# Unread products of the identity on TensorE between the steps of a rotation

## The chip, the cores and the metric

The kernel runs on one core of a Trainium2 chip. The metric is the device time of one execution in microseconds; the median of three runs of the kernel before is 2110.49 us. One execution was also recorded by the profiler.

## The reference

The input x has the shape 4 x 512 x 288, the condition 4 x 288, all in float32. Four blocks are computed in turn:

- a rotation: U is the Q of a QR decomposition of P (288 x 64); per batch a skew matrix is made from silu(cond) @ W.T + b, and its matrix exponential R (64 x 64) rotates the part of x that lies in the span of U: x + ((x U) R - x U) U^T;
- two transformer blocks with modulation by the condition (layer norm, attention with 16 heads of 18, a feed-forward of 1152), the second with a layer norm of each head's queries and keys;
- a third one whose feed-forward is a mixture of four experts, of which each token uses two.

The change lies in the first block and in the start of the first attention.

## The kernel before

**The QR decomposition** is an elimination of 64 steps on the Gram matrix, written out as a Python loop over columns (lines 560 to 576). Two chains run in it. `gram_step(i)` copies row i of X to all 64 partitions by a product with one column of the identity (`to_all`, g_bc), and VectorE makes from it the reciprocal rn, the multipliers Fm and the update of X; ScalarE takes a root (Nm) and GpSimd a product (Rh). `sign_step(i)` does the same with row i of Wt (w_bc) and fixes the signs: six small operations of VectorE, of which the last writes Wt. The loop calls gram_step(i + 1) ahead of to_all and sign_step(i), so that g_bc runs one column ahead. Both rows are put into tiles of PSUM with the tag "big": two banks wide, two buffers in all, used in turn. Of each tile only the first bank is used here.

**Beside it** the loop advances three generators. `main` (`skew_and_exp`) transposes W (p_WT), multiplies (p_v), builds the skew matrices, and from column 33 on runs nine steps of a series (p_ser) and sixteen squarings (p_sq), one per column, each a group of 64 x 64 products and one operation of VectorE. `side` transposes x (p_t), projects it (p_zP), and later does the first modulations (p_mod, p_modT). `fills` clears buffers. In the whole loop the instructions keep the order of the program on each engine. TensorE takes its products in that order.

**Behind the loop** p_E and p_Q finish Q; `rotate(0)` applies the rotation to batches 0 and 1 in six parts (p_RU, p_EU, and four times p_xr with VectorE's sums into x). `head_biases(0)` makes bias columns (p_qkb). `normalize` computes the layer norm of batch 0 on VectorE and ScalarE, `project(0)` transposes and makes queries, keys and values (p_t, p_qk, p_v), with parts of `rotate(1)` between, and sends queries and keys through memory into the layout of heads. Then ten steps of `maxima` (LOOK = 10) run ahead of the attention's loop: each makes two products p_s of 32 rows by 512 columns in one "big" tile, and VectorE takes their maximum. The last parts of `rotate(1)` lie between these steps. The attention's loop, the feed-forwards and the experts follow.

A dependence between engines is a wait on a semaphore that counts the finished instructions of an engine. An instruction of TensorE that waits holds all that stand behind it.

Of the kernel before, what the change touches and what calls it, by code (L numbers as in the profile page):

```python
# [33 lines left out]
D = 64  # L34
# [13 lines left out]
def cond_seq_kernel(ctx: ExitStack, tc: tile.TileContext, a: dict, out: bass.AP):  # L48
# [16 lines left out]
    matmul, transpose = InOrder(nc.tensor).matmul, InOrder(nc.tensor).transpose  # L65
# [10 lines left out]
    blocks = ctx.enter_context(ExitStack())  # L76
    fixed = blocks.enter_context(tc.tile_pool(name="fixed", bufs=1))

    def pmm(name):
        return ps.tile([128, 512], F32, tag="mm", name=name, bufs=3)  # L80

    def pbig(name):
        return ps.tile([128, 2, 512], F32, tag="big", name=name)

    def pacc(name):
        return ps.tile([128, 512], F32, tag="acc", name=name, bufs=1)
# [17 lines left out]

    ident = const.tile([128, 128], F32, name="ident")
    make_identity(nc, ident)
    ones = const.tile([1, 128], F32, name="ones")
    nc.gpsimd.memset(ones, 1.0)
    eps6 = const.tile([128, 1], F32, name="eps6")
# [60 lines left out]
    def to_columns(name, r):  # L170

        p = pmm(f"p_{name}")
        for m in range(NQ):
            w = min(QP, QK - m * QP)
            matmul(p[0:w, m:m + 1], r[:, m * QP:m * QP + w], ones[:, 0:1], start=True, stop=True)
        t = const.tile([QP, NQ], F32, name=name)
        nc.gpsimd.memset(t, 0.0)
        scalar.copy(t[:, 0:NQ - 1], p[0:QP, 0:NQ - 1])
        scalar.copy(t[0:w, NQ - 1:NQ], p[0:w, NQ - 1:NQ])
        return t  # L180
# [21 lines left out]
    def head_biases(l):  # L202
        QB[l] = to_columns(f"qkb{l}", WA[l][3])
        if l != 1:
            vector.tensor_mul(QB[l], QB[l], scol)
# [155 lines left out]
    with tc.tile_pool(name="l0", bufs=1) as l0, tc.tile_pool(name="l0w", bufs=2) as l0w, \  # L361
# [24 lines left out]
        Hs = l0.tile([D, D], F32, name="Hs")  # L386

        def to_all(name, i, src):
            p = pbig(name)[:D, 0, :src.shape[-1]]
            matmul(p, ident[:D, i:i + 1].to_broadcast([D, D]), src, start=True, stop=True)  # L390
            return p

        def gram_step(i):
            bc = to_all(f"g_bc{i}", i, X[:, i:i + D + 1])
            rn = l0w.tile([D, 1], F32, tag="rn", name=f"rn{i}")
            vector.reciprocal(rn, bc[:, 0:1])
            vector.scalar_tensor_tensor(Fm[:, i:i + 1], X[:, i:i + 1], rn, minus[:, i:i + 1], ALU.mult, ALU.mult)
            vector.scalar_tensor_tensor(X[:, i + 1:i + D + 1], bc[:, 1:], Fm[:, i:i + 1],
                                        X[:, i + 1:i + D + 1], ALU.mult, ALU.add)
            scalar.activation(Nm[:, i:i + 1], bc[:, 0:1], AF.Sqrt, scale=0.25)  # L400
            nc.gpsimd.tensor_mul(Rh[:, i:i + 1], Fm[:, i:i + 1], Nm[:, i:i + 1])

        def sign_step(i, bc):

            h = Hs[:, i:i + 1]
            vector.tensor_scalar(h, bc[:, 0:1], 0.0, 0.5, ALU.is_lt, ALU.subtract)
            if i == D - 1:
                return
            st = l0w.tile([D, 4], F32, tag="st", name=f"st{i}")
            den, rec, num, c = (st[:, n:n + 1] for n in range(4))  # L410
            vector.tensor_scalar(den, bc[:, 0:1], h, Nm[:, i:i + 1], ALU.mult, ALU.subtract)
            vector.scalar_tensor_tensor(num, Wt[:, i:i + 1], h, Rh[:, i:i + 1], ALU.mult, ALU.add)
            vector.reciprocal(rec, den)
            vector.scalar_tensor_tensor(c, num, rec, minus[:, i:i + 1], ALU.mult, ALU.mult)
            vector.scalar_tensor_tensor(Wt[:, i + 1:], bc[:, 1:], c, Wt[:, i + 1:], ALU.mult, ALU.add)
# [145 lines left out]
        for i in range(D):  # L561
            column[0] = i
            if i + 1 < D:
                gram_step(i + 1)
            bc = to_all(f"w_bc{i}", i, Wt[:, i:])
            beside = i >= 6 and (i < 15 or i >= 18)
            next(main, None)
            if beside:
                next(side, None)
            sign_step(i, bc)  # L570
            next(main, None)
            if beside:
                next(side, None)
            next(fills, None)
            if i == 27:

                WA.append(load_attn(0, "L1_cond_W_qkv", "L1_cond_b_qkv", "L1_cond_W_proj", "L1_cond_b_proj"))
# [17 lines left out]
                                    Hs.rearrange("p (o d) -> p o d", o=1).to_broadcast([D, B, D]), ALU.mult, ALU.mult)  # L595
        pt = pmm("p_Q")
        matmul(pt[:D, :C], Em, At, start=True, stop=True)
        vector.tensor_scalar_mul(QT, pt[:D, :C], rnorm)
        scalar.copy(XD, X[:, D:])


    def rotate(n):

        ts = []
        for h in range(2):
            p = pmm(f"p_RU{2 * n + h}")
            matmul(p[:D, :C], Es[:, 2 * n + h, :], QT, start=True, stop=True)
            t = work.tile([128, C], F32, tag="gated", name=f"RU{2 * n + h}", bufs=3)
            scalar.mul(t[:D], p[:D, :C], rnorm)
            ts.append(t)  # L610
        yield 0.6
        e = work.tile([128, C], F32, tag="gate", name=f"EU{n}")
        p = pmm(f"p_EU{n}")
        for h in range(2):
            matmul(p[h * D:(h + 1) * D, :C], XD, ts[h][:D], start=True, stop=True)
        scalar.copy(e, p[:, :C])
        yield 0.6
        for j in range(NT):
            ps = pmm(f"p_xr{2 * n}_{j}"), pacc(f"p_xr{2 * n + 1}_{j}")
            for h in range(2):  # L620
                r = slice(h * D, (h + 1) * D)
                matmul(ps[h][:, :C], zP[r, n, j * 128:(j + 1) * 128], e[r], start=True, stop=True)
            for h in range(2):
                xb = x[2 * n + h][:, j, :]
                vector.tensor_add(xb, ps[h][:, :C], xb)
            yield 0.6
# [6 lines left out]
    def normalize(l, part, b, after=None):  # L633


        xn = []
        mv = work.tile([128, NT, 2], F32, tag="mv", name=f"mv{l}_{part}_{b}")
        for j in range(NT):
            while after is not None and (after, j) not in done:
                yield False  # L640
            s6 = work.tile([128, 6], F32, tag="s6", name=f"s6_{l}_{part}_{b}_{j}", bufs=4)
            vector.bn_stats(s6, x[b][:, j, :])
            vector.bn_aggr(mv[:, j, :], s6)
            yield True

        r = work.tile([128, 2, NT], F32, tag="rstd", name=f"rstd{l}_{part}_{b}")
        y, t, var = r[:, 0, :], r[:, 1, :], mv[:, :, 1]
        scalar.activation(y, var, AF.Ln, bias=eps6)
        scalar.activation(y, y, AF.Exp, scale=-0.5)
        yield True  # L650
        vector.scalar_tensor_tensor(t, var, 1e-6, y, ALU.add, ALU.mult)
        vector.tensor_mul(t, t, y)
        vector.tensor_scalar(t, t, -0.5, 1.5, ALU.mult, ALU.add)
        vector.tensor_mul(y, y, t)
        yield True
        for j in range(NT):
            t = work.tile([128, C], F32, tag="xn", name=f"xn{l}_{part}_{b}_{j}", bufs=8)
            vector.tensor_scalar(t, x[b][:, j, :], mv[:, j, 0:1], y[:, j:j + 1], ALU.subtract, ALU.mult)
            xn.append(t)
            yield True  # L660
        XN[l, part, b] = xn
# [345 lines left out]
    with tc.tile_pool(name="attn", bufs=2) as at:  # L1007
# [90 lines left out]
        def maxima(G, step):  # L1098

            n, g = divmod(G, NG)  # L1100
            j, hp = divmod(step, 2)
            p = pbig(f"p_s{G}_{step}")
            for i in range(2):
                r = slice((2 * hp + i) * HS, (2 * hp + i + 1) * HS)
                matmul(p[:, i, :], Q[n % 2][r, g, j * 128:(j + 1) * 128], K[n % 2][r, g, :], start=True, stop=True)
            vector.tensor_reduce(M[G % 2][:, j, 2 * hp:2 * hp + 2, HD:HD + 1], p, AX.X, ALU.max)
# [155 lines left out]
            yield from route(b)  # L1262

        E, ready, PO, S, there, norms = [], [], [None], {}, set(), {}
        for _ in rotate(0):
            pass
        head_biases(0)
        norm = normalize(0, 0, 0)
        for _ in norm:
            pass  # L1270
# [3 lines left out]
        for cost in project(0, norm):  # L1274
            next(norm1, None)
            sent = sent or cost is None
            if sent and cost == 0.95:
                next(rest, None)
        norm = norm1
        for t in range(LOOK):  # L1280
            maxima(*divmod(t, 8))
            if t == 8:
                take_maxima(0)
            next(norm, None)
            next(rest, None)
# [212 lines left out]
```

## Time and profile before

| | |
|---|---|
| median of 3 runs | 2110.49 us (2103.7 to 2111.6) |
| the profiled execution | 2122.64 us, span 2120.9 us |
| TensorE busy | 1933.4 us, 91% of the span |
| VectorE busy | 933.8 us |
| ScalarE busy | 777.1 us |
| mean granted clock of TensorE | 0.933 |
| columns of the rotation | 7.6 us (first reciprocal) to 148.6 us (last w_bc) |
| first product of maxima | 194.8 us |

A row of the timeline has the start and the length in us, the engine, the line, the operation, what it writes and reads, rows and columns of the array, the shape, and the number of instructions merged; in brackets the idle time of the engine just before it and what ended that. Nearly all instructions are recorded at line 60, that of a helper, so groups are read by the names of tiles. A product in float32 is recorded as two MATMULs, one per pass; a transpose as one. The granted clock is 1.00 at full and 0.50 at half speed.

### The profile page before, as it was taken

Reading aid. Unit: us, or ns where it says so; the run is one execution under the profiler, and the core shown is the slowest. Engines: PE = TensorE matmul, PEld = TensorE weight load, DVE = VectorE, ACT = ScalarE, POOL = GpSimd, SP = SyncE. Lnnn points to the kernel's source line nnn. Section 1 sums busy time; section 2 is a strip of 40 time slices with the busy share of each in tenths; the row PEclk is TensorE's granted clock in tenths of the full one; section 3 lists DMA queues with packets and bytes.
Section 4 is the critical chain, followed back from the end, with each engine's and each line's share of the span. In section 5 each row is a group of like instructions: output and inputs, shape, how many; then the busy total and the mean of one; then the engine's idle time right before and its main releaser. Section 6 shows DMA issues by size and latency. Waiting matters only on the chain. (4 is left out here: it accounts for less than half of the span.)

```text
span 2120.9 us, 26102 instructions
## 1 busy us (share of the span) xinstructions
PE 1933.4 (91%) x10200; PEld 936.0 (44%) x10200; DVE 933.8 (44%) x1974; ACT 777.1 (37%) x1159; POOL 251.3 (12%) x361
## 2 busy tenths in 40 slices
PE   7778989999999999899999999998987899999997
PEld 4553322343433434334234343333322367777775
DVE  6774535526256263552643626355577134111111
ACT  5111444434345354443543434434444222112111
POOL 1000001000001020110100000000010122332322
PEclk9556899999999999989999999999999689999999
DMA  3211125122031121511213112161221355666563
GB/s 95 70 39 45 34 65 160 26 56 76 16 75 41 52 79 45 127 46 25 88 27 77 48 51 81 21 135 31 81 51 58 111 196 178 203 207 223 182 216 94
DMA packets 89418, 187.21 MB, mean 88 GB/s; under 512 B 25453, under 2 KB 50456, under 8 KB 86802
## 3 DMA queue, kind: packets, MB, share of 16 engines
q1 hardware_dynamic: 77462, 103.39, 18.8%
q0 software_dynamic: 11248, 79.79, 11.6%
q10 hardware_dynamic: 584, 2.36, 0.4%
q8 instruction: 80, 1.31, 0.3%
q14 instruction: 44, 0.36, 0.1%
HBM read 152.49 MB, written 55.45 MB: 98 GB/s over the span
## 5 line engine op out<-in xcount | busy, mean ns | idle before, releaser
L60 ACT ACTIVATE e<-p_st 128x1024 f32<-128x1024 f32 x384 | 392.7, 1023 | 692.1 <-PE p_st L60 687.8
L60 DVE TENSOR_REDUCE store<-p_s 128x2 f32<-128x1024 f32 x384 | 470.2, 1225 | 385.1 <-PE p_st L60 334.0
L60 PE MATMUL p_s<-store 32*128 32x512 f32 x1536 | 452.6, 664 | 79.7 <-DVE store L60 76.9
L60 PE MATMUL p_st<-store 32*128 32x512 f32 x1536 | 449.8, 664 | 0.9 <-DVE store L60 0.9
L60 PEld LDWEIGHTS p_s<-store 32*128 32x128 f32 x1536 | 122.7, 190 | 312.5 <-DVE store L60 221.4
L60 PE MATMUL p_av<-e,store 128*32 128x512 f32 x1536 | 213.5, 629 | 2.2 <-ACT e L60 2.2
L60 PE MATMUL p_he<-hTe,store 128*128 128x256 f32 (+1 forms) x1026 | 200.1, 404 | 4.2 <-DVE hTe L60 4.2
L60 PE MATMUL p_ye<-store,hide 128*128 128x288 f32 x684 | 175.0, 415 | 7.1 <-ACT hide L60 7.1
L60 ACT ACTIVATE hide<-p_he,store 128x256 f32<-128x256 f32 x171 | 68.5, 471 | 281.8 <-PE p_he L60 281.8
L60 PEld LDWEIGHTS p_he<-hTe,store 128*128 128x128 f32 (+1 forms) x1026 | 147.6, 191 | 53.1 <-issue 30.5
L691 POOL TENSOR_TENSOR x<-x,gated 128x288 f32<-128x288 f32 x80 | 63.4, 793 | 848.0 <-DVE gated L60 848.0
L60 PE MATMUL p_qk<-hT,wqk 128*126 128x512 f32 (+1 forms) x360 | 163.9, 626 | 0.0
L60 PE MATMUL p_h<-hT,w 128*128 128x512 f32 (+1 forms) x432 | 156.7, 618 | 5.2 <-DVE store L60 5.2
L60 PEld LDWEIGHTS p_ye<-store,hide 128*128 128x128 f32 x684 | 130.3, 193 | 46.9 <-ACT hide L60 10.9
L60 PE MATMUL p_y<-w,hid 128*128 128x288 f32 x576 | 141.8, 407 | 0.0
L60 DVE TENSOR_TENSOR gated<-p_y,gate 128x288 f32<-128x288 f32 x32 | 14.6, 457 | 285.8 <-PE p_y L60 285.8
L60 PEld LDWEIGHTS p_st<-store 32*128 32x128 f32 x1536 | 119.5, 189 | 12.4 <-issue 9.3
L60 PEld LDWEIGHTS p_y<-w,hid 128*128 128x128 f32 x576 | 108.8, 190 | 35.5 <-issue 6.1
L60 PEld LDWEIGHTS p_h<-hT,w 128*128 128x128 f32 (+1 forms) x432 | 60.7, 189 | 99.7 <-issue 83.6
L60 PE MATMUL p_o<-wp,oc 126*128 126x288 f32 (+1 forms) x288 | 101.2, 475 | 1.3 <-DVE oc L60 1.3
L60 PEld LDWEIGHTS p_qk<-hT,wqk 128*126 128x126 f32 (+1 forms) x360 | 47.8, 179 | 98.7 <-issue 98.5
L60 DVE COPY hTe<-p_te 128x512 f32<-128x512 f32 x19 | 13.1, 690 | 172.9 <-PE p_tf L60 127.8
(248 smaller groups left out, 1736.6 us busy)
## 6 DMA issues: line engine op xcount, KB each, us to landing
store<-qd SPq DMA_DIRECT2D x96, 144.0 KB
qd<-stage SPq DMA_DIRECT2D x48, 252.0 KB
od<-o SPq DMA_DIRECT2D x192, 36.0 KB
rd<-rd SPq DMA_DIRECT2D x12, 576.0 KB
oc<-od SPq DMA_DIRECT2D x24, 252.0 KB
rb<-rd SPq DMA_DIRECT2D x24, 252.0 KB
etab<-in_L_cond_w_dram SPq DMA_DIRECT2D x4, 1296.0 KB
etab<-in_L_cond_w_dram SPq DMA_DIRECT2D x8, 576.0 KB
```

Of the source, the lines that this page charges most:

```text
L60: ins = f(*args, **kw)
L691: nc.gpsimd.tensor_add(x[b][:, j, :], x[b][:, j, :], t)
```

## The change

A function `keep_warm(bank, n)` multiplies the identity by the identity, taken up to four times side by side, and writes n columns (in pieces of at most 512) to a bank of PSUM that nothing reads. It is called

- in each column of the loop, behind sign_step and the generators, with 384 or 256 columns, into the second bank of the tile that holds w_bc;
- behind p_Q (256), behind each part of rotate(0) (256), behind head_biases(0) (five of 512);
- in project(0) behind two pieces of the values (512), and once behind it (512);
- behind each of the ten steps of maxima (128, from the sixth on 256), into a tile of the tag "mm".

```diff
+    def keep_warm(bank, n):
+
+        while n > 0:
+            w = min(n, 512)
+            matmul(bank[:, :w].rearrange("p (o m) -> p o m", m=128), ident, ident_wide[:, :w // 128, :], start=True, stop=True)
+            n -= w
...
+    ident_wide = ident.rearrange("p (o m) -> p o m", o=1).to_broadcast([128, 4, 128])
...
         def to_all(name, i, src):
-            p = pbig(name)[:D, 0, :src.shape[-1]]
+            t = pbig(name)
+            p = t[:D, 0, :src.shape[-1]]
             matmul(p, ident[:D, i:i + 1].to_broadcast([D, D]), src, start=True, stop=True)
+            free[0] = t[:, 1]
             return p
+
+        free = [None]
...
             bc = to_all(f"w_bc{i}", i, Wt[:, i:])
             beside = i >= 6 and (i < 15 or i >= 18)
+            warm = free[0]
             next(main, None)
             if beside:
                 next(side, None)
...
+            keep_warm(warm, 384 if i < 3 or i >= 52 or 29 <= i < 33 else 256)
             next(fills, None)
...
         matmul(pt[:D, :C], Em, At, start=True, stop=True)
+        keep_warm(pbig("warm0")[:, 0], 256)
         vector.tensor_scalar_mul(QT, pt[:D, :C], rnorm)
...
+        warm = pbig("warm1")
         for _ in rotate(0):
-            pass
+            keep_warm(warm[:, 0], 256)
         head_biases(0)
+        keep_warm(warm[:, 0], 5 * 512)
...
             if sent and cost == 0.95:
                 next(rest, None)
+                keep_warm(warm[:, 1], 512)
+        keep_warm(warm[:, 1], 512)
         norm = norm1
         for t in range(LOOK):
             maxima(*divmod(t, 8))
+            keep_warm(pmm(f"warm2_{t}"), 256 if t > 4 else 128)
```

## The prediction

> **What bounds the kernel now.** I read the page's rows of forty slices first, then the busy time by stretches of the opening, then the timeline of single columns. Each slice is 53 us.
>
> ```profile
> PE   7778989999999999899999999998987899999997
> PEclk9556899999999999989999999999999689999999
> ```
>
> TensorE is busy nearly everywhere, and the granted clock is low in the second to fourth slice, that is in the rotation and just behind it. Nothing before or behind the opening is touched by the change, so the opening is read by stretches. The columns are the length, then PE, PEld, DVE, ACT and POOL busy, then the clock.
>
> ```profile
> 29.00:46.20 17.20, 14.84 (x107) 7.89 (x109) 13.90 (x78) 7.57 (x21) 1.66 (x12) 1.00 0.13 38
> 46.20:80.00 33.80, 25.21 (x108) 13.50 (x100) 25.84 (x145) 9.02 (x28) 2.93 (x16) 0.50 0.45 110
> 80.00:148.00 68.00, 51.18 (x563) 39.65 (x563) 55.36 (x293) 9.03 (x45) 7.10 (x34) 0.50 0.13 31
> 149.00:176.00 27.00, 19.87 (x53) 10.04 (x54) 12.13 (x46) 6.15 (x15) 0.00 (x0) 0.50 0.00 0
> 196.40:227.00 30.60, 28.94 (x78) 9.16 (x76) 17.69 (x22) 1.23 (x2) 0.26 (x1) 0.50 0.00 1
> ```
>
> The reader is to see that the clock is at half for 130 us (46.2 to 175.9) and again for 31 us, though TensorE is shown busy for 75% and 95% of those stretches. Which of this costs time is a second question. In the rotation (64 columns, 7.6 to 148.6) VectorE does nine small operations per column, and the timeline of one column shows who waits:
>
> ```profile
> 142.93 0.21 DVE L60 SCALAR_TENSOR_TENSOR Wt<-w_bc,st,Wt 64x4 f32<-64x4 f32 x1
> 143.06 0.15 DVE L60 RECIPROCAL rn<-g_bc 64x1 f32<-64x1 f32 x1
> 143.29 0.34 PE L60 MATMUL w_bc<-Wt,ident 64*64 64x4 f32 x2 [0.49 <-DVE rn L60]
> ...
> 144.08 0.48 PE L60 MATMUL g_bc<-X,ident 64*64 64x65 f32 x2 [0.45 <-ACT Nm L60]
> ...
> 144.69 0.21 DVE L60 SCALAR_TENSOR_TENSOR Wt<-w_bc,st,Wt 64x3 f32<-64x3 f32 x1
> 144.83 0.15 DVE L60 RECIPROCAL rn<-g_bc 64x1 f32<-64x1 f32 x1
> ```
>
> The broadcast row g_bc for the next column is computed at 144.08, while VectorE is still in the sign step; so when Wt ends at 144.90 the reciprocal rn has its input and follows at once (1.77 us from rn to rn). Even at half clock TensorE's round trip is under VectorE's work. In columns that also add a series or squaring result the step is 2.1 us, again all VectorE. Over the 62 steps from the second to the last rn (8.99 to 146.64) 137.7 us pass; the waits of rn on g_bc sum to 12.3 us in the whole rotation. So a faster TensorE has at most about 12 us to win there. What happens if g_bc is late is seen where long products stand ahead of it:
>
> ```profile
> 63.17 1.97 PE L60 MATMUL p_zP<-xT,hT 96*64 96x512 f32 x4
> ...
> 65.08 0.47 PE L60 MATMUL g_bc<-X,ident 64*64 64x65 f32 x2
> 65.59 0.16 DVE L60 RECIPROCAL rn<-g_bc 64x1 f32<-64x1 f32 x1 [0.59 <-PE g_bc L60]
> ```
>
> g_bc starts as p_zP is through, and VectorE idles for it: rn follows 0.51 us behind g_bc's start.
>
> **The change part by part.**
>
> **The 64 products in the rotation.** Each writes the second bank of the tile whose first bank holds w_bc(i), and is emitted behind sign_step(i). In the instruction list of the changed program each such product waits for a VectorE count, and the count is that of Wt(i), the last reader of w_bc(i): the wait is kept per tile, not per bank. Behind it in TensorE's queue stands g_bc(i+2), whose own wait (on ScalarE's Nm) is met long before. So g_bc(i+2), which before ran during sign_step(i), now runs behind the end of sign_step(i) and behind the product. rn, X, w_bc(i+1) and all the rest of the column wait for that.
>
> The price of a product comes from the weight loads of p_qk, one per pass of 512 columns, two passes per product, on either side of the clock's change at 175.9:
>
> ```profile
> 174.51 0.34 PEld L60 LDWEIGHTS p_qk<-hT,wqk 128*126 128x126 f32 x1 [0.52 <-issue]
> 175.36 0.34 PEld L60 LDWEIGHTS p_qk<-hT,wqk 128*126 128x126 f32 x1 [0.52 <-issue]
> ...
> 176.51 0.19 PEld L60 LDWEIGHTS p_qk<-hT,wqk 128*126 128x126 f32 x1 [0.24 <-issue]
> 176.94 0.19 PEld L60 LDWEIGHTS p_qk<-hT,wqk 128*126 128x126 f32 x1 [0.24 <-issue]
> ```
>
> A pass takes 0.85 us at half clock and 0.43 at full. A product of 256 columns is then 0.85 or 0.43 us, of 384 1.28 or 0.64, of 512 1.71 or 0.86. The new round trip from the end of Wt to rn: 0.15 until TensorE starts (Wt ends 142.93+0.21, w_bc at 143.29), the product, g_bc 0.47 (0.33 at full clock, at 30.79), 0.04 to rn. That is 1.51 us at half clock, 0.95 at full. From rn to the end of Wt VectorE needs 1.84 (143.06 to 144.90). A column becomes 3.35 us at half clock, 2.79 at full; with 384 columns 3.78 and 3.00. The series and squaring results (0.40), the products for them and the other work on TensorE now lie beside this round trip and cost nothing more; if it were gone they would cost what they cost before.
>
> **Does the clock rise?** The nearest rows are TensorE's own. From 196.4 to 227 it is busy 95% of the time with products on 64 of 128 rows and stays at half. From 60.7 to 67.6 p_zP (96 rows) runs about 80% of the time and the clock does not rise. It rose at 29 (four p_WT took 1.07 us before, 0.64 behind; no clock is on record before that) behind six us of 126- and 128-row transposes that filled about 85% of each column, and at 175.9 behind dense p_t and p_qk; it was lost at 46.2 in columns whose p_v uses 4 array columns. At half clock a column with a 256 product has 0.85 of 3.35 us of whole array and the series' products on a quarter of it, worth about 0.45 us more: 1.3 of 3.35, near 0.4 of the array, less than the stretches that stayed low. The Trainium skill's page "TensorE: Matmul & The Clock Gate" (Part 1) counts otherwise: a busy window of about 3.4 us gives full clock, and only an idle one of that length takes it away. By that rule TensorE, with no idle gap above 1.5 us between 46 and 149, should have been at full clock already; the trace has 0.50 there. I take the trace: full clock in some five columns after 29 us as before, half in the rest. By the rule it would be full clock from the tenth column on.
>
> By the trace: 45 columns of 256 at 3.35 = 151, 17 of 384 at 3.78 = 64, five columns at full clock -3, the column with the modT transposes +2: 214 against 137.7, +76 us. By the rule: 45 x 2.79 + 17 x 3.00 = 177, the first nine at half clock +6, +1: 184, +46 us.
>
> **Behind the rotation.** The last two products of 384 stand ahead of w_bc(63) and of p_E: +3 us at half clock. warm0 and the six products between rotate(0)'s parts fill gaps of 0.5 us (waits on QT, RU, EU and the sums) and stick out by about 0.35 each, the last by its whole 0.85: +3 (at full clock all of this is -2 with the chain's own products halved). The five of 512 stand where TensorE waits from 165.1 to 169.8 for the normalization: 4.3 us at full clock fit; at half clock 8.5 would stick out by 4, but p_xr just ahead (two side by side fill the array, with the new ones between near 0.8 of the time) and these five themselves raise the clock. Then p_t and p_qk up to 175.9 start at full clock: -2. The three of 512 beside the second rotation: +1.7, less 0.8 idle: +1. Maxima:
>
> ```profile
> 200.66 1.33 PE L60 MATMUL p_xr<-EU,hT 64*128 64x288 f32 x4
> 200.81 1.23 DVE L60 TENSOR_REDUCE store<-p_s 128x2 f32<-128x1024 f32 x1 [1.23 <-PE p_s L60]
> 201.93 2.08 PE L60 MATMUL p_s<-store 32*128 32x512 f32 x4
> ```
>
> Four steps of 3.27 us (p_xr and p_s at half clock) fall to VectorE's 2.1 (the maximum 1.23 and two sums 0.82) at full clock with 128 columns added; the six behind win 2, p_bv and the first p_st 3: -9. If the clock is not held here it is +4 instead.
>
> Sum: 76 + 3 + 3 - 2 + 1 - 9 = +72 on the profiled execution's 2122.6 us (2120.9 of span): 2195. That execution was 12.1 us above the median of the runs, 2110.5: **2183** there.
>
> **The rivals.**
>
> **Full clock through the rotation.** For it: the widths are larger exactly where TensorE has least to do, and it was held from 29 to 46 with about 0.35 of the array. Against it: 0.23 to 0.3 of the array at full clock in the later columns, less than where it was lost. It gives 46 + 1 - 2 - 2 + 1 - 9 = +35: 2145.
>
> **Hidden products, and the clock held: faster.** If the products ran in the gap between g_bc and w_bc (0.5 to 0.66 us in the timeline, against 0.43 for 256 columns) the column would stay as it is, rn's 12.3 us of waits would shrink by perhaps 8, and with -6 on the chain from p_Q to the sums and -10 behind it this would be -24: 2087. It needs a product that is free to start before Wt(i) has ended, or an exposed round trip of under 0.39 us a column (24 over 62). Against it: the wait on Wt(i) in the instruction list, and the order of the queue, in which nothing behind a blocked product can start.
>
> **The change does nothing.** The added waits and the clock's gains cancel, or the round trip lies beside other VectorE work: only in the 26 series columns is there any, 0.40 us. Little speaks for it.
>
> **How the numbers follow.** Half clock in the rotation 0.65 (2168 to 2203), full clock through most of it 0.23 (2130 to 2165), faster 0.08, no change 0.04. The range 2134 to 2203 leaves out about the last two and a corner of the second. About 0.5% (11 us) is what a measurement of this kernel can tell from no change. Slower 0.88, same 0.04, faster 0.08.
>
> **What would show it.** rn should wait on g_bc in all columns, 0.9 to 1.6 us each, 50 to 90 us in total instead of 12.3; w_bc's product should wait on Wt; the last rn should stand at 200 to 230 us (half) or near 190 (full) instead of 146.6; the clock at half in most of it and at full from the normalization to past the maxima; maxima every 2.1 us in the first four steps. A last rn near 140 would make the prediction wrong, and so would a clock of 0.5 over the maxima, in size.

## The result, and the profile after

The changed kernel takes 2190.43 us (median of 4 runs, 2185.02 to 2198.64), against 2109.15 us before (4 runs): ratio 1.0386, 95% interval 1.0344 to 1.0427. The forecast was 2183, with a range of 2134 to 2203. In the rows below PE is TensorE and PEld its weight loads, DVE is VectorE, ACT ScalarE and POOL GpSimd.

The rows of the forty slices (55 us each now) show the low clock in the second to fifth slice, one more than before:

```profile
PE   6778899899999999989999999999997889999998
PEclk9655699899999999999999999999999989999999
```

The stretches of the opening, cut where the clock changes (columns as in the prediction; the first entry is the stretch, the last two are the DMA engines' share and GB/s):

```profile
43.70:74.40 30.70, 22.74 (x144) 11.60 (x142) 17.39 (x95) 9.60 (x27) 1.84 (x11) 1.00 0.05 17
74.40:160.00 85.60, 63.33 (x330) 35.32 (x330) 42.00 (x224) 7.07 (x29) 4.79 (x25) 0.50 0.17 43
160.00:240.00 80.00, 61.11 (x408) 34.98 (x405) 38.39 (x198) 8.48 (x36) 4.86 (x23) 0.50 0.11 26
240.00:255.30 15.30, 14.76 (x34) 5.74 (x33) 3.18 (x12) 1.84 (x5) 0.00 (x0) 0.50 0.00 0
255.30:289.00 33.70, 33.45 (x113) 14.91 (x112) 11.21 (x40) 9.93 (x20) 0.00 (x0) 1.00 0.25 69
289.00:311.00 22.00, 22.00 (x96) 8.76 (x96) 16.23 (x21) 0.00 (x0) 0.26 (x1) 1.00 0.01 2
```

The rotation now runs to 240, not 148.6, and from 74.4 on at half clock. VectorE's share is what to look at: 38.4 of 80 us, where it had 55.4 of 68. It waits. Two rows of the waits between 9 and 237 us say for whom:

```profile
DVE rn L60 <- PE g_bc L60: 100.3, 63, 2.9
PEld w_bc L60 <- DVE Wt L60: 79.8, 61, 2.2
```

The numbers are the total in us, the number of waits and the longest. The kernel before had, between 9 and 148 us:

```profile
DVE rn L60 <- PE g_bc L60: 12.1, 21, 2.0
```

So rn waited in 21 columns, and now it does in every one. (The second row above is the weight load of the product, which writes a tile named w_bc.) The timeline of one column in the series, at half clock; "..." stands for rows left out:

```profile
152.68 0.23 DVE L60 SCALAR_TENSOR_TENSOR Wt<-w_bc,st,Wt 64x23 f32<-64x23 f32 x1
152.84 0.41 DVE L60 SCALAR_TENSOR_TENSOR ser<-p_ser,S 128x256 f32<-128x256 f32 x1
152.97 0.50 PEld L60 LDWEIGHTS w_bc<-ident 128*128 128x128 f32 x2 [1.09 <-DVE Wt L60]
152.97 1.22 PE L60 MATMUL w_bc<-ident 128*128 128x256 f32 x2 [0.90 <-DVE Wt L60]
...
154.12 0.47 PE L60 MATMUL g_bc<-X,ident 64*64 64x65 f32 x2
...
154.63 0.16 DVE L60 RECIPROCAL rn<-g_bc 64x1 f32<-64x1 f32 x1 [1.39 <-PE g_bc L60]
```

Wt ends at 152.91, the product starts 0.06 us later, g_bc starts 1.15 us later, rn 0.51 us behind that. TensorE had been idle for 0.90 us ahead of the product: the gap is there, but the product can't use it.

From 289 on, the maxima, at full clock:

```profile
294.57 1.23 DVE L60 TENSOR_REDUCE store<-p_s 128x2 f32<-128x1024 f32 x1 [0.18 <-PE p_s L60]
...
295.56 1.13 PE L60 MATMUL p_s<-store 32*128 32x512 f32 x4
...
296.73 1.23 DVE L60 TENSOR_REDUCE store<-p_s 128x2 f32<-128x1024 f32 x1 [0.21 <-PE p_s L60]
```

One step is 2.16 us, where it was 3.27. From the first p_s to the first exponential the changed kernel takes 22.0 us, the one before 31.0.

By landmarks, after against before, in us: last rn +89.9, p_E +93.3, the first statistics of the normalization +94.5, first p_v +92.3, first p_s +94.3, first exponential +85.3. The two profiled spans differ by 62.4 only; the other 23 were won back behind the first exponential, where the change adds nothing. There the clock's record has 126 us at half clock in the profiled execution of before and 80 in that of the changed kernel; half of these 46 us is 23 (an estimate that takes all of that work to wait for TensorE). Executions of one kernel differ by such amounts: four of the changed one span 2183.3 to 2196.9, and the profiled one is the shortest, while that of before was 12 us above its median. The medians differ by 81.3.

### The profile page after: what moved, and what is told of

Read it like the earlier page. It is cut to its first block, busy times and chain, and to the rows that moved or that the text cites. A ratio compares the mean times of both kernels' runs of the same rounds, so it can differ in the third digit from the quotient of the medians.

```text
span 2183.3 us, 26392 instructions
## 1 busy us (share of the span) xinstructions
PE 1981.5 (91%) x10378; PEld 958.6 (44%) x10378; DVE 935.9 (43%) x1974; ACT 776.6 (36%) x1159; POOL 251.0 (11%) x361
## 5 line engine op out<-in xcount | busy, mean ns | idle before, releaser
L60 PE MATMUL p_s<-store 32*128 32x512 f32 x1536 | 440.9, 646 | 79.5 <-DVE store L60 77.3
L60 PE MATMUL p_st<-store 32*128 32x512 f32 x1536 | 439.7, 649 | 0.9 <-DVE store L60 0.9
L60 PE MATMUL p_he<-hTe,store 128*128 128x256 f32 (+1 forms) x1026 | 200.2, 405 | 4.2 <-DVE hTe L60 4.2
L60 PEld LDWEIGHTS p_he<-hTe,store 128*128 128x128 f32 (+1 forms) x1026 | 147.8, 191 | 53.1 <-issue 30.6
L60 PE MATMUL w_bc<-ident 128*128 128x256 f32 (+1 forms) x128 | 80.9, 732 | 55.3 <-DVE Wt L60 55.1
L60 PE MATMUL p_o<-wp,oc 126*128 126x288 f32 (+1 forms) x288 | 91.5, 438 | 1.3 <-DVE oc L60 1.3
```

The source lines that it names most:

```text
L60: ins = f(*args, **kw)
```

## The experiments

All times are medians; the ratios are to runs of the kernel before on the same chip.

**behind: the loop's products left out.**

```diff
-            keep_warm(warm, 384 if i < 3 or i >= 52 or 29 <= i < 33 else 256)
```

> The changed kernel without the 64 products inside the columns of the rotation; all products behind it stay. Queue theory (a product waits for Wt, and g_bc of the next column stands behind it): the last rn is back at 146.6 us, the products from p_Q to the bias columns cost 1 us, the maxima win 9 us by the full clock, so about 2101 us, 0.4% under the 2109 of before. Rival (the products behind the rotation share the loss): over 2115 us.

Measured: 2103.49 us (12 runs), ratio 0.9981 (0.995 to 1.0011); the last rn at 145.5, the first exponential 9.7 us earlier than before. So the whole loss lies in the loop; the products behind it shorten their stage, but by less than the totals resolve, as the interval takes in 1. The stretch from the first p_s to the first exponential, before and here:

```profile
194.80:225.80 31.00, 29.60 (x75) 9.22 (x76) 16.49 (x21) 0.03 (x1) 0.26 (x1) 0.53 0.03 7
```

```profile
194.10:216.00 21.90, 21.90 (x96) 8.73 (x96) 16.21 (x20) 0.00 (x0) 0.26 (x1) 1.00 0.00 1
```

**loop_only: only the loop's products.**

```diff
-        keep_warm(pbig("warm0")[:, 0], 256)
...
-            keep_warm(warm[:, 0], 256)
+            pass
...
-        keep_warm(warm[:, 0], 5 * 512)
...
-                keep_warm(warm[:, 1], 512)
-        keep_warm(warm[:, 1], 512)
...
-            keep_warm(pmm(f"warm2_{t}"), 256 if t > 4 else 128)
```

> Only the 64 products inside the columns; none behind the rotation. Queue theory: the last rn stays at 236.6 us, the first p_s finds half clock again, the ten maxima take 31 us as before, so about 2109 + 90 = 2199 us. Rival (what lies behind costs too): under 2180 us.

Measured: 2202.18 us (4 runs), ratio 1.0441 (1.0389 to 1.0493); last rn at 234.6; from the first p_s to the first exponential 29.8 us at a mean clock of 0.59. With behind it splits the change: about +94 from the loop, -5 to -12 from the rest.

**narrow: the same wait and place, two columns.**

```diff
-            keep_warm(warm, 384 if i < 3 or i >= 52 or 29 <= i < 33 else 256)
+            matmul(warm[:, :2], ident, ident[:, :2], start=True, stop=True)
```

> The products inside the columns write 2 columns instead of 256 or 384; place and wait stay, and all behind the rotation stays. Queue theory: g_bc still starts only behind the end of Wt, so a column is 1.84 (VectorE) + 0.15 + 0.35 (two short passes with their weight loads) + 0.51 (g_bc to rn) = 2.85 us; last rn near 186 us, in all about 2109 + 39 - 8 = 2140 us. Rival (the loss is TensorE's time for the products, not the wait): last rn near 147 us, in all about 2101 us.

Measured: 2154.21 us (4 runs), ratio 1.0236 (1.0179 to 1.0292); last rn at 200.2, +54. With next to no columns streamed through the array, more than half of the loss is there. This execution ran its whole rotation at half clock (its p_v take 1.02 us, against 0.59 at full), where the kernel before had 17 us at full, so a small part of the 54 may be the clock's: the three columns with p_v take 4.03 us, the others near 3.0. A column of it:

```profile
143.50 0.23 DVE L60 SCALAR_TENSOR_TENSOR Wt<-w_bc,st,Wt 64x20 f32<-64x20 f32 x1
...
143.87 0.50 PEld L60 LDWEIGHTS w_bc<-ident 128*128 128x128 f32 x2 [0.96 <-DVE Wt L60]
143.88 0.59 PE L60 MATMUL w_bc<-ident 128*128 128x2 f32 x2
...
144.39 0.47 PE L60 MATMUL g_bc<-X,ident 64*64 64x65 f32 x2
...
144.91 0.16 DVE L60 RECIPROCAL rn<-g_bc 64x1 f32<-64x1 f32 x1 [0.85 <-PE g_bc L60]
```

g_bc starts 0.51 us behind the start of a product of two columns. That is two weight loads of the identity (0.50 in the timeline), and the expectation had 0.35 for the whole of it. This column takes 3.06 us, most take 2.94 to 3.00, and the mean of 62 is 3.08; expected were 2.85, hence 2154 instead of 2140.

**free: the same products, waiting for nothing.**

```diff
+                keep_warm(p[:, 4 * D:], 256)
                 return p[:, :4 * D]
...
-            keep_warm(warm, 384 if i < 3 or i >= 52 or 29 <= i < 33 else 256)
+            if i < 34 or i >= 59:
+                keep_warm(pacc(f"free{i}"), 384 if i < 3 or i >= 52 or 29 <= i < 33 else 256)
```

Up to column 33 only the tile differs from the changed kernel: width and place in the order are the same. From column 34 on the product stands behind the series' or squaring products, in their bank.

> The products inside the columns keep their widths (256 in place of 384 in columns 52 to 58) but write the accumulator's bank, alone up to column 33, then beside the series' products, so that none waits for VectorE. Queue theory: the columns without much other work go back to near 2 us, those with transposes or projections stay near 3.6 as TensorE at half clock is full there; last rn 165 to 185 us, in all 2120 to 2140 us. Rival (TensorE's time for the products is the loss, the wait adds nothing): last rn 215 to 237 us, over 2170 us.

Measured: 2124.95 us (9 runs), ratio 1.0086 (1.0054 to 1.0119); last rn at 164.8, +18. The wait of rn on g_bc is 16.9 us in all, and g_bc no longer follows Wt through a product:

```profile
142.71 1.22 PE L60 MATMUL p_sq<-ident 128*128 128x256 f32 x2
...
143.34 0.22 DVE L60 SCALAR_TENSOR_TENSOR Wt<-w_bc,st,Wt 64x10 f32<-64x10 f32 x1
...
143.86 0.29 PEld L60 LDWEIGHTS g_bc<-X,ident 64*64 64x64 f32 x2 [0.65 <-issue]
143.97 0.42 DVE L60 SCALAR_TENSOR_TENSOR sq<-sq,p_sq 128x256 f32<-128x256 f32 x1 [0.41 <-PE p_sq L60]
...
144.37 0.16 DVE L60 RECIPROCAL rn<-g_bc 64x1 f32<-64x1 f32 x1
```

The product starts ahead of Wt's end, so a column is 2.78 us instead of 3.59. The first 33 columns are the cleanest comparison: rn of column 33 starts at 77.2 before, at 78.2 here and at 121.8 in the changed kernel. So the same products cost 1 us without the wait and 45 with it; full clock, which stands here from 21.2 to 72.4, helps by a part of that. What is left of the loss comes later, where TensorE at half clock has no idle time left, and the squaring result, which shares the product's tile, waits for it:

```profile
126.70:165.00 38.30, 38.04 (x267) 25.10 (x266) 27.59 (x138) 3.82 (x22) 3.77 (x17) 0.50 0.12 28
```

Between 120.2 and 127.0 the clock was at full once more; the two columns that start there, at 121.8 and 124.0, took 2.13 and 3.90 us, no longer than before (2.54 and 4.21).

**swap: g_bc ahead of the product** (`width` gives 384 or 256 as the removed line does).

```diff
-        def gram_step(i):
+        def gram_step(i, behind=None):
             bc = to_all(f"g_bc{i}", i, X[:, i:i + D + 1])
+            if behind is not None:
+                keep_warm(behind, width(i - 2))
...
-                gram_step(i + 1)
+                gram_step(i + 1, warm)
+            else:
+                keep_warm(warm, width(i - 1))
...
-            keep_warm(warm, 384 if i < 3 or i >= 52 or 29 <= i < 33 else 256)
...
+        keep_warm(warm, 384)
         for _ in main:
```

> The changed kernel with each product of the rotation one place later in TensorE's order: behind g_bc of the next column but one, ahead of the next w_bc. Width and the wait for Wt stay. Queue theory: g_bc runs early again and rn follows Wt; now w_bc stands behind the product, 0.15 + 1.15 + 0.35 us after Wt, where VectorE needs it 0.65 to 0.9 us after Wt, so a column at half clock is 1.65 + 1.20 = 2.9 us (3.4 with 384), about 3.9 with transposes; last rn near 205 us, in all about 2160. Rival (the place in the queue is of no weight, the product's own time is): last rn at 230 us or more, 2185 or more.

Measured: 2166.7 us (5 runs), ratio 1.0296 (1.0242 to 1.035); last rn at 210.6. One place in the order is worth 26 us of the rotation, with the same products, the same wait and as long a full clock (31 us of the rotation in both). The size of the gain was overrated by a few us: in the columns with modulations rn waits after all.

```profile
152.20 1.22 PE L60 MATMUL w_bc<-ident 128*128 128x256 f32 x2
...
153.48 0.29 PE L60 MATMUL w_bc<-Wt,ident 64*64 64x19 f32 x1
...
153.92 0.15 DVE L60 TENSOR_SCALAR Hs<-w_bc 64x1 f32<-64x1 f32 x1 [0.89 <-PE w_bc L60]
...
155.80 0.48 PE L60 MATMUL g_bc<-X,ident 64*64 64x65 f32 x2
...
156.31 0.16 DVE L60 RECIPROCAL rn<-g_bc 64x1 f32<-64x1 f32 x1 [0.83 <-PE g_bc L60]
```

Hs waits for the w_bc that stands behind the product, as expected. But p_sq and p_mod stand behind that w_bc, and the next g_bc behind them: rn waits 0.83 us more, and the column is 4.0 us.

**lift: 2560 columns in four columns of the rotation.**

```diff
-            keep_warm(warm, 384 if i < 3 or i >= 52 or 29 <= i < 33 else 256)
+            keep_warm(warm, 5 * 512 if 34 <= i < 38 else 384 if i < 3 or i >= 52 or 29 <= i < 33 else 256)
```

> The changed kernel with 2560 columns instead of 256 in columns 34 to 37 of the rotation, to raise the clock there; all else as in the changed kernel. Theory that the clock follows how much of the array is used: it rises in the first or second of these columns, and is lost within 7 us after column 38, as columns of 256 use about a quarter of the array at full clock; columns from 40 on take 3.6 us again, last rn near 250 us. Rival (a busy window raises the clock and only an idle one takes it away): full clock to the end of the rotation, columns of 2.95 us, last rn near 233 us.

Measured: 2223.84 us (one run); last rn at 261.2, where 250 was expected. Ten of these 11 us lie ahead of the first wide column: column 34 starts at 135.8, and at 125.8 in the changed kernel, though up to there the two are the same program; here the first 34 columns all ran at half clock (more on this below). The clock's record begins with the rise at 147.4, inside the first wide column, and has the loss at 174.7. The wide columns at full clock, what follows until the loss, and the half clock behind:

```profile
147.40:169.50 22.10, 17.97 (x101) 8.51 (x101) 5.87 (x30) 0.49 (x3) 0.55 (x3) 1.00 0.00 1
169.50:174.70 5.20, 2.45 (x41) 1.83 (x39) 3.92 (x20) 0.33 (x2) 0.37 (x2) 1.00 0.00 0
174.70:205.00 30.30, 28.01 (x215) 15.47 (x214) 15.59 (x80) 3.88 (x16) 1.47 (x8) 0.50 0.15 35
```

A wide column takes 6.78 us, of which ten passes of 0.43 fill the whole array, 0.63 of the time. The columns of 256 behind them (the first takes 2.93 us) lose the clock 5.2 us later, with TensorE shown busy for 47% and no idle gap above 1.4 us. So in this one execution the products of the change were too few to hold the clock in these columns, even once it was there.

**maxima_only: only the products beside the values and the maxima.**

```diff
-            keep_warm(warm, 384 if i < 3 or i >= 52 or 29 <= i < 33 else 256)
...
-        keep_warm(pbig("warm0")[:, 0], 256)
...
-            keep_warm(warm[:, 0], 256)
+            pass
...
-        keep_warm(warm[:, 0], 5 * 512)
```

> Only the products beside the values, behind the projection and in the ten steps of maxima; none in or ahead of rotate(0) and none at the bias columns. Queue theory: the rotation and the chain behind it take the time of before; the clock, at full by the projection's own products, is held over the maxima, which take 9 us less; about 2099 us against 2108, and 1 us better than with the products from p_Q on. Rival (the products at the bias columns are what brings the clock to the maxima): half clock there and no gain.

Measured: 2104.75 us (12 runs), ratio 0.9972 (0.9937 to 1.0006). The clock was held:

```profile
196.90:218.80 21.90, 21.90 (x96) 8.73 (x96) 16.22 (x21) 0.00 (x0) 0.26 (x1) 1.00 0.00 1
```

The first exponential comes 6.9 us earlier than before; of the 9 us of the maxima, the three products of 512 ahead of them cost 1.9 (the first p_s is 2.1 late). The products from p_Q to the bias columns win about 1.5 us more: in behind the first exponential is 9.7 us earlier than before, but 1.1 of that is there at the last rn already, where the two kernels are the same. The rival expectation, that the clock needs the products at the bias columns, is out. The expectation that those products cost 1 us was wrong in sign, though by less than the totals of behind and this run (2103.49 and 2104.75) can tell. Neither version is told from the kernel before by its total; both beat the changed one.

## Why the prediction was right

**The wait and the order** (right). The prediction's step was that the product waits for Wt and g_bc stands behind it, so that the round trip comes onto the path. The product writes the second bank of its tile and Wt reads the first, and yet 61 weight loads of the product waited for Wt (79.8 us). narrow (the wait with almost no streaming, +54 us at the last rn), free (the streaming without the wait, +18, and only 1 of the 45 us up to column 33) and swap (-26 by one place in the order) show it, each with its own edit. rn waits in every column: 1.05 us in those at full clock, 1.39 to 1.82 in most at half, 2.15 in most of those with 384, and 100 us in all. Forecast were 0.9 to 1.6 each and 50 to 90 in all.

**The column's size** (0.25 us too small at half clock, 0.16 at full). 3.60 and 2.95 us were measured, 3.35 and 2.79 forecast. The term that was mis-sized is the product: 0.85 us was taken from the spacing of p_qk's passes, where the weight loads lie beside the stream before them. Here nothing streams before them, and 1.15 us pass from the start of the product to that of g_bc, 0.30 more; at full clock it is 0.63 instead of 0.43. The start of the product was misread the other way: the 0.15 us from Wt to w_bc in the prediction's timeline lie ahead of a product that waited for rn, as its bracket says, and the start behind Wt took 0.06. Over 52 steps at half clock and ten at full this makes about 15 us too little; longer columns (the first of 4.97, those with p_mod of 3.69) add about 2, and five more columns at full clock than forecast take 3 off. Together they are the 14 us by which the rotation's forecast of +76 fell short of +90.

**The clock** (right in its choice, half clock in most of the rotation; the rest is luck). Half clock stood from 74.4 to 255.3; full clock lasted ten columns (43.8 to 74.5), not five. How long it lasts differs between executions of the same instructions. In loop_only, whose rotation is the same program, it was there from 35.0 to 72.4; in lift, the same up to column 33, not at all. The products p_v of these columns show it, in the changed kernel and in lift (shortest, median and longest in ns, then first and last start):

```profile
L60 PE MATMUL p_v<-WT,scT x24: 586/586/587, 61.6 to 67.9; 96*4 96x504 f32 x16, 97*4 97x504 f32 x8
L60 PE MATMUL p_v<-WT,scT x24: 1000/1023/1044, 68.9 to 76.9; 96*4 96x504 f32 x16, 97*4 97x504 f32 x8
```

This alone moves the rotation's end by up to 10 us, more than the 7 by which the forecast of the total missed. By the rule of the Trainium skill's page "TensorE: Matmul & The Clock Gate" (Part 1), as the prediction cites it, only an idle window of about 3.4 us takes full clock away, and the last rn would have stood near 190. It stood at 236.6. In the kernel before, full clock was lost 1.7 us after the products on half of the rows began (194.8 to 196.5), with TensorE busy throughout, and in lift with no idle gap above 1.4 us; in lift TensorE was also shown busy for 38.5 of the 39.3 us from 44.0 to 83.3, all at half clock. So neither TensorE's busy share nor its idle gaps set the clock here. The array's use fits these losses better, but it isn't shown to be the rule: the same columns, with the same use, rose at 43.7, at 35.0 or not at all.

**Behind the rotation** (right but for small terms). p_E came 3.4 us later against before than the last rn (forecast +3), the chain to the statistics added 1.2 (forecast +3), p_t and p_qk -2.2 (forecast -2), the three of 512 +1.9 (forecast +1), the maxima -9.0 (forecast -9). At the first exponential this is +85, where the sum said +72; the median of all runs says +81.

**The rivals.** Full clock through the rotation is out by the record. For hidden products and a gain, the condition, a product that is free to start before Wt has ended, was made in free; even so the rotation took 18 us more, as TensorE at half clock was full in the later columns. Nothing cancelled: the loop costs about 94 us and the rest wins 5 to 12.

## What to carry to other kernels

Work that is to fill a gap must be free to start in it: write it where no pending reader is, and look in the instruction list for what its wait is and what stands behind it in its queue. If an engine is off the path, as TensorE was in this rotation, ask first what its clock could win (here at most the 12 us that rn waited) before any work is spent on that clock. Where TensorE is the bound, as in the first maxima, filling it for a few us before and between does hold the clock and takes 9 us of 31, of which 2 are paid for the filling ahead. Which of these products are needed was not tried, and the total did not show the gain.

## What the runs showed of the hardware

The clock did not follow TensorE's busy share. Products on half of the rows stayed at half clock for 30.6 us at 95% busy in the kernel before (196.4 to 227); in loop_only the same stage had 3.4 us at full in between (301.3 to 304.7), so this too varies. With 128 to 512 columns of the identity ahead of and between these products, full clock held through the stage in the changed kernel, in behind and in maxima_only (21.9 us at 1.00). In the columns of the rotation it was held for 22 us while 0.63 of the array's time was filled, and lost 5.2 us after columns began that fill about a quarter (an estimate from rows, columns and times of the products in lift).

The weight loads of a product show in its time when nothing streams ahead: a float32 product of two columns took 0.51 us at half clock, about its two loads (0.50), and one of 256 columns 1.15 us, where its passes alone would take 0.85.
